# Attention in a two-layer graph network on one core: the order of the heads, and which of them goes into the shared third PSUM bank when

## The chip, the cores and the metric

The kernel runs on one core of one Trainium2 chip. Its time is the device time of one execution in microseconds (us). Before the change the median of three executions is 2405.86 us (2405.43 to 2407.07).

A core has several engines that run side by side, each with its own queue: TensorE (PE in the profile) multiplies matrices and writes its results to PSUM[...]; VectorE (DVE), ScalarE (ACT) and GpSimd (POOL) work element by element; SyncE (SP) issues the transfers (DMAs). An engine takes its instructions in the order in which they were written. Between engines, a semaphore tells one that another has finished.

## The reference, cut to what matters

There are 128 graphs of 128 nodes with 512 features each. Layer 0 is graph attention with 8 heads of 64 units, layer 1 a hypergraph convolution with a hidden width of 1024; each is added to its input and normalized. The change is in layer 0, in the product of the attention weights with the features:

```python
feats = jnp.einsum('bnf,hfu->bhnu', X, W)
e_self = jnp.einsum('bhnu,hu->bhn', feats, a_self)
e_neigh = jnp.einsum('bhnu,hu->bhn', feats, a_neigh)
dense = jax.nn.leaky_relu(e_self[..., :, None] + e_neigh[..., None, :], negative_slope=0.2)
dense = dense + NEG_BIG * (1.0 - A[:, None, :, :])
att = jax.nn.softmax(dense, axis=-1)
out = jnp.einsum('bhij,bhju->bhiu', att, feats) + b[None, :, None, :]
...
x = _layernorm(x + _L0_gnn_ref(x, adj, ...), axis=-1)
x = _layernorm(x + _L1_gnn_ref(x, adj, ...), axis=-1)
```

## The kernel before

**Pairs.** The 128 graphs are taken two at a time: 64 pairs, p = 0 to 63. All work of a pair is cut into steps, small functions such as `attend_pair(p, s)`, where `s` holds the pair's tiles. A step is declared with a lag and a time: `@step(2, 24.1, since=1, until=LAST)` puts it at (p + 2) x 38.6 + 24.1 on a clock that serves only for ordering. At the end of the kernel all steps of all pairs are sorted by that number and called; so several pairs are under way at once, and the order of each engine's queue is the order of the calls. The start and the last pairs have times and functions of their own.

**Attention of one pair.** The scores of both graphs lie in one tile `nb`, half a graph (four heads) at a time: GpSimd adds the mask (`masked`, line 589), ScalarE applies the leaky ReLU (line 605), VectorE takes the largest (line 611), ScalarE the exponential (line 619). The product needs the exponentials transposed. For that a graph's half of `nb` is written to DRAM (`e_write`, line 623: ed<-nb) and read back by blocks of 32 rows (`e_read`, line 631: four transfers eb<-ed), and VectorE transposes the blocks (`e_transpose`, line 640: eT<-eb), four heads in one instruction. There are four of these per pair: first graph's heads 0 to 3 and 4 to 7 (times 16.6 and 16.65), second graph's heads 0 to 3 and 4 to 7 (21.5 and 21.55).

**The product.** For each graph and head, `attend_pair` (line 703) multiplies the transposed exponentials `eT` with the features `ft`, which have a column of ones appended, so that each head gives 64 columns of results and one column with the sum of the weights: 65 columns. Each head is done in two matmuls of 64 output rows, and in the profile each of these is two records. A bank holds 512 fp32 columns, so seven heads (455 columns). Heads 0 to 6 of the first graph go into `pav_0`, those of the second into `pav_1`, and head 7 of both (`HB`) into a shared third bank, `pav_2`. `pav_2` is reserved in an earlier step (`attend_rest`, time 20.9), ahead of the first product of layer 1's second weights (pyX, time 21.0); `pav_0` and `pav_1` are reserved in `attend_pair`. All banks come from one pool of eight, `psum`. The order of the matmuls is: head 7 of both graphs, then heads 0 to 6 of the first, then heads 0 to 6 of the second.

**The evictions.** `attended_pair` (time 26.3, lines 734 and 735) takes the reciprocal of each sum and multiplies the results with it into `y`, in three instruction pairs on VectorE: `pav_2` first, then `pav_0`, then `pav_1`. `residual` (line 751) applies the ReLU and adds the input, `moments` (lines 759 and 760) and `rstds` (line 767, GpSimd) make the statistics of the layer norm, `first_shift` and `first_output` (lines 785 to 794, ScalarE) apply it to `y`, and `propagate` (pz, on TensorE) is the first use of `y`.

**Around the product.** On TensorE the last part of the feature product of the next pair (pfX, pfW) stands ahead of the attention, and products of layer 1's second weights (pyX, pyY, pyW) stand behind it; the helper of those matmuls is line 97. On VectorE, `f_sum` (line 509), `spread_rows` (line 542) and `x_transpose` (line 385) of other pairs stand between the last `e_transpose` and the evictions. Pairs 0 and 63 use `attend` and `attended`, with four heads to a bank, in place of the functions that are changed.

Of the kernel before, what the change touches and what calls it, by code (L numbers as in the profile page):

```python
# [20 lines left out]
def kernel(  # L21
# [67 lines left out]
    def bank(name):  # L89
        return psum.tile([P, HALF], F32, tag="bank", name=name)  # L90
# [120 lines left out]
    for i in range(2):  # L211
        t = const.tile([P, 2, H, UW + 1], F32, name=f"ft{i}")
# [103 lines left out]
    def step(lag, time, since=0, until=PAIRS):  # L316

        def keep(fn):
            steps.append((lag, time, fn.__name__, range(since, until), fn, ()))
            return fn  # L320
        return keep
# [364 lines left out]
    HB = H - 1  # L686

    @step(2, 20.9, since=1, until=LAST)
    def attend_rest(p, s):
        s["pav", 2] = bank(f"pav_{p}_2")  # L690

    @step(2, 24.1, since=1, until=LAST)
    def attend_pair(p, s):

        rest = s["pav", 2][:, :2 * (U + 1)].rearrange("p (g u) -> p g u", g=2)
        to = [(rest[:, g, :], g, HB) for g in range(2)]
        for g in range(2):
            t = s["pav", g] = bank(f"pav_{p}_{g}")
            to += [(t[:, h * (U + 1):(h + 1) * (U + 1)], g, h) for h in range(HB)]
        for t, g, h in to:  # L700
            for c in range(2):
                rows = slice(c * P // 2, (c + 1) * P // 2)
                nc.tensor.matmul(  # L703
                    t[rows], s["eT"][:, g, h, rows], s["ft"][:, g, h, 2:], start=True, stop=True,
                )
# [17 lines left out]
    @step(2, 26.3, since=1, until=LAST)  # L723
    def attended_pair(p, s):
        y = s["y"] = work.tile([P, 2, F], F32, tag="y", name=f"y_{p}")
        rden = small.tile([P, 2, H], F32, tag="rden2", name=f"rden_{p}", bufs=2)
        heads = y.rearrange("p g (h u) -> p g h u", h=H)
        rest = s["pav", 2][:, :2 * (U + 1)].rearrange("p (g u) -> p g u", g=2)
        for r, t, dst in [(rden[:, :, HB], rest, heads[:, :, HB, :])] + [
            (rden[:, g, :HB],  # L730
             s["pav", g][:, :HB * (U + 1)].rearrange("p (h u) -> p h u", h=HB),
             heads[:, g, :HB, :]) for g in range(2)
        ]:
            nc.vector.reciprocal(r, t[:, :, U])
            nc.vector.tensor_tensor(
                dst, t[:, :, :U], r.unsqueeze(2).to_broadcast(list(dst.shape)), op=ALU.mult
            )
# [538 lines left out]
```

## Time and profile before

| What | Value |
|---|---|
| median of three executions | 2405.86 us (2405.43 to 2407.07) |
| the profiled execution's own time | 2395.3 us |
| its span, first to last instruction | 2393.4 us |
| mean granted TensorE clock | 0.996 of full speed |
| PE (TensorE matmul) | busy 99% of the span |
| DVE (VectorE) | 87% |
| POOL (GpSimd) | 76% |
| ACT (ScalarE) | 64% |
| matmul records of attention, line 703 | 3968, for 62 pairs |
| reciprocals and multiplications of attended_pair | 186 each |
| bytes moved | 347.09 MB, mean 145 GB/s |

The profile is of one execution. Its page gives each engine's busy time, the chain of work that ended last, and the costliest groups of instructions. The trace behind it can be asked for more: the waits (who waited for whom, with total, number and longest), and the timeline, which lists instructions in order of time as start, length, engine, line, operation, what is written and read, and how many were merged in the row; in brackets stands how long the engine was idle before, and what ended that. A busy share is of the engine's whole span; the ends of matmuls are modelled, so a busy PE is not PE at its peak.

### The profile page before, as it was taken

How to read it: one execution, taken by the hardware profiler on the slowest of the kernel's cores; microseconds unless marked ns; L12 is line 12 of the kernel's file. 1: busy time of each engine (PE TensorE's matmuls, PEld its weight loads, DVE VectorE, ACT ScalarE, POOL GpSimd, SP SyncE). 2: the span in 40 equal slices, each digit the busy share in tenths (PEclk: the TensorE clock that was granted, in tenths of full speed). 3: DMA queues.
4: the chain of work that ended last, by engine and by line, in shares of the span. 5: the costliest groups of instructions: out<-in, count | busy, mean ns of one | idle time of the engine just before them, and what ended most of it. 6: DMA issues, size and time to landing. Idle time of an engine off the chain costs nothing.

```text
span 2393.4 us, 80729 instructions
## 1 busy us (share of the span) xinstructions
PE 2360.8 (99%) x32309; PEld 2026.8 (85%) x32309; DVE 2089.6 (87%) x4456; ACT 1528.5 (64%) x4481; POOL 1825.6 (76%) x2060
## 2 busy tenths in 40 slices
PE   7899999999999999999999999999999999999998
PEld 6788887888888888888888888888888888888886
DVE  7989888898898898898898888988988988988975
ACT  4565765756667667667667666666676676676662
POOL 5877786777877877877877778778778778778774
PEclk9999999999999999999999999999999999999999
DMA  6555454555554555555545555544545555555541
GB/s 197 133 148 150 143 144 134 159 143 147 151 148 144 149 148 148 151 143 154 144 142 157 141 147 155 146 146 147 150 143 153 147 150 139 148 156 140 149 128 37
DMA packets 431134, 347.09 MB, mean 145 GB/s; under 512 B 151440, under 2 KB 380328, under 8 KB 430760
## 3 DMA queue, kind: packets, MB, share of 16 engines
q1 hardware_dynamic: 427288, 337.46, 49.5%
q8 instruction: 256, 4.19, 0.7%
q10 hardware_dynamic: 3472, 4.47, 0.6%
q14 instruction: 118, 0.97, 0.2%
HBM read 239.08 MB, written 102.73 MB: 143 GB/s over the span
## 4 chain that ended last, share of the span: by engine, by line
PE 89%; DMA 4%; DVE 3%; ACT 1%; POOL 1%; issue 1%; SPq 1%; DVEq 0%; POOLq 0%; ACTq 0%
PE phX L97 17%; PE pyX L97 17%; PE pfX L97 8%; PE pyW L97 8%; PE phW L97 8%; PE pav L703 5%; PE phY L97 4%; PE pz L97 4%; PE pfW L97 4%; PE pq L97 4%; PE pyY L97 4%; PE pfY L97 2%; DMA ed<-nb 1%; PE pd L97 1%; DMA nb<-rd 1%
## 5 line engine op out<-in xcount | busy, mean ns | idle before, releaser
L344 ACT COPY py<-pyX 128x257 f32<-128x257 f32 x189 | 70.7, 374 | 538.5 <-PE pyX L97 465.6
L97 PEld LDWEIGHTS phX<-zS,w_sb 128*64 128x64 f32 x6144 | 350.6, 137 | 36.3 <-POOL ft L742 23.1
L97 PE MATMUL phX<-zS,w_sb 128*64 128x128 f32 x6144 | 373.4, 273 | 2.6 <-ACT ph L344 2.6
L904 POOL TENSOR_TENSOR sq<-sq 128x512 f32<-128x512 f32 (+2 forms) x384 | 343.9, 896 | 20.1
L589 POOL TENSOR_TENSOR nb<-nb,neg 128x512 f32<-128x512 f32 x256 | 319.9, 1284 | 23.1 <-DMA nb<-rd 12.7
L605 ACT ACTIVATE nb<-nb,ft 128x128 f32<-128x128 f32 x1020 | 325.1, 392 | 13.7 <-POOL nb L589 13.7
L619 ACT ACTIVATE nb<-nb,nm 128x128 f32<-128x128 f32 x1024 | 319.4, 392 | 4.2 <-DVE nm L611 4.0
L767 POOL TENSOR_TENSOR rso<-veo,mhalf 128x2 f32<-128x2 f32 x63 | 44.2, 701 | 338.4 <-DVE veo L765 338.4
L97 PE MATMUL pyX<-w_sb,hS 128*64 128x257 f32 x2016 | 245.1, 380 | 0.0
L97 PE MATMUL pyX<-w_sb,h 128*64 128x257 f32 x2016 | 243.7, 379 | 0.5 <-ACT py L344 0.5
L97 PE MATMUL pyW<-w_sb,hS 128*64 128x256 f32 x2016 | 243.3, 378 | 0.0
L881 ACT ACTIVATE h<-h,vecs 128x128 f32<-128x128 f32 x768 | 239.4, 394 | 2.0 <-DVE h L866 1.4
L611 DVE TENSOR_REDUCE nm<-nb 128x4 f32<-128x512 f32 x256 | 175.2, 684 | 48.8 <-ACT nb L605 46.2
L97 PEld LDWEIGHTS pyX<-w_sb,h 128*64 128x64 f32 x2016 | 173.7, 136 | 46.2 <-ACT py L344 0.9
L97 PEld LDWEIGHTS pyW<-w_sb,hS 128*64 128x64 f32 x2016 | 174.7, 136 | 43.6 <-issue 0.3
L742 POOL TENSOR_TENSOR ft<-ft,b_bc 128x512 f32<-128x512 f32 x128 | 203.9, 1613 | 6.1 <-ACT ft L533 6.1
L97 PEld LDWEIGHTS pyX<-w_sb,hS 128*64 128x64 f32 x2016 | 168.7, 137 | 38.7 <-issue 0.8
L640 DVE STREAM_TRANSPOSE eT<-eb 128x512 f32<-128x512 f32 x252 | 163.5, 685 | 5.7 <-DMA eb<-ed 4.7
L805 DVE SCALAR_TENSOR_TENSOR o<-y,b_bc 128x512 f32<-128x512 f32 x128 | 164.7, 1325 | 0.0
L1006 DVE SCALAR_TENSOR_TENSOR y<-y,rsh,bw_bc 128x512 f32<-128x512 f32 x126 | 150.1, 1229 | 14.9 <-POOL rsh L1002 14.9
L469 POOL TENSOR_TENSOR hS<-h 128x512 f32<-128x512 f32 x126 | 162.1, 1287 | 0.0
L892 ACT ACTIVATE sq<-h 128x512 f32<-128x512 f32 x256 | 160.6, 629 | 2.1
(178 smaller groups left out, 5672.4 us busy)
## 6 DMA issues: line engine op xcount, KB each, us to landing
nb<-rd SPq DMA_DIRECT2D x127, 512.0 KB, 5.6
ed<-nb SPq DMA_DIRECT2D x126, 512.0 KB, 3.4
eb<-ed SPq DMA_DIRECT2D x504, 128.0 KB, 2.9
x<-in_x_dram SPq DMA_DIRECT2D x64, 512.0 KB, 4.0
out_dram<-o SPq DMA_DIRECT2D x63, 512.0 KB, 2.9
xb<-in_x_dram SPq DMA_DIRECT2D x248, 128.0 KB, 5.5
a<-in_adj_dram SPq DMA_DIRECT2D x64, 128.0 KB, 2.4
w<-in_adj_dram SPq DMA_DIRECT2D x128, 64.0 KB, 5.0
```

The costliest lines, as they stand in the source:

```text
L97: nc.tensor.matmul(to[rows], lhs[:, rows], rhs, start=start, stop=stop, skip_group_check=True)
L469: engine.tensor_tensor(t[:, i], in0, in1, op=op)
L589: nc.gpsimd.tensor_tensor(t, t, neg[:, :, None, :].to_broadcast([P, NB, HH, B]), op=ALU.add)
L605: nc.scalar.activation(t, t, AF.Prelu, bias=s["ft"][:, g, h, 0:1], alpha=SLOPE)
L611: nc.vector.tensor_reduce(s["nm"][:, g, hs], scores(p, s, g, hs).rearrange("p b h j -> p h b j"), AX.XY, ALU.max, negate=True,)
L619: nc.scalar.activation(t, t, AF.Exp, bias=s["nm"][:, g, h:h + 1])
L640: nc.vector.transpose(s["eT"][:, g, hs, :].rearrange("p h (b i) -> p h b i", b=NB), s["eb", g][:, :, hs, :].rearrange("p b h j -> p h b j"),)
L742: nc.gpsimd.tensor_tensor(t, t, b0_bc.rearrange("p (h u) -> p h u", h=H), op=ALU.add)
L805: nc.vector.scalar_tensor_tensor(s["o"][:, g, :], s["y"][:, g, :], 2.0, b2_bc, op0=ALU.mult, op1=ALU.add)
L881: nc.scalar.activation(dst[:, k, :], src[:, k, :], AF.Relu, bias=b1_sb[:, c:c + 1])
L892: nc.scalar.activation(s["sq"][:, g, q * KH // 2:(q + 1) * KH // 2, :], hid(s, g, q), AF.Square, scale=DH ** -0.5,)
L904: nc.gpsimd.tensor_tensor(t[:, :n, :], t[:, :n, :], t[:, n:2 * n, :], op=ALU.add)
```

## The change

The early step now reserves the bank of the first graph's heads 0 to 6 (`pav_0`), and `attend_pair` reserves `pav_1` and `pav_2`. The matmuls are issued in the order of the heads: heads 0 to 6 of the first graph into `pav_0`, its head 7 into `pav_2`, then heads 0 to 6 of the second graph into `pav_1`, and its head 7 into `pav_2`. The evictions follow the same order: `pav_0`, `pav_1`, and `pav_2` last. The number, the shapes and the operands of all instructions stay. Steps of pairs 0 and 63 are not touched.

```diff
     @step(2, 20.9, since=1, until=LAST)
     def attend_rest(p, s):
-        s["pav", 2] = bank(f"pav_{p}_2")
+        s["pav", 0] = bank(f"pav_{p}_0")
...
-        to = [(rest[:, g, :], g, HB) for g in range(2)]
+        to = []
         for g in range(2):
-            t = s["pav", g] = bank(f"pav_{p}_{g}")
+            t = s["pav", g]
             to += [(t[:, h * (U + 1):(h + 1) * (U + 1)], g, h) for h in range(HB)]
+            to.append((rest[:, g, :], g, HB))
...
-        for r, t, dst in [(rden[:, :, HB], rest, heads[:, :, HB, :])] + [
+        for r, t, dst in [
             (rden[:, g, :HB],
              s["pav", g][:, :HB * (U + 1)].rearrange("p (h u) -> p h u", h=HB),
              heads[:, g, :HB, :]) for g in range(2)
-        ]:
+        ] + [(rden[:, :, HB], rest, heads[:, :, HB, :])]:
```

At the head of `attend_pair` stands the new reservation:

```python
s["pav", 1], s["pav", 2] = (bank(f"pav_{p}_{g}") for g in (1, 2))
```

## The prediction

> **What bounds the kernel now.** I read the page first, then the waits of TensorE, then the timeline of one steady pair, and then the places where the waits of TensorE in attention lie.
>
> ```profile
> span 2393.4 us, 80729 instructions
> ...
> PE 2360.8 (99%) x32309; PEld 2026.8 (85%) x32309; DVE 2089.6 (87%) x4456; ACT 1528.5 (64%) x4481; POOL 1825.6 (76%) x2060
> ...
> PE 89%; DMA 4%; DVE 3%; ACT 1%; POOL 1%; issue 1%; SPq 1%; DVEq 0%; POOLq 0%; ACTq 0%
> ```
>
> TensorE is busy for 99% of the span and carries 89% of the chain that ended last. So a change of order can gain only where TensorE waits, and can lose only where it makes TensorE wait. The list of TensorE's waits, cut to those that touch attention (line 703) and the next consumer of its result (pz), has per row the total, the number and the longest:
>
> ```profile
> PE pz L97 <- ACT y L794: 4.0, 1, 4.0
> PE pav L703 <- DVE eT L640: 4.0, 2, 2.3
> ...
> PE pav L703 <- POOL hS L469: 0.6, 1, 0.6
> ```
>
> Three waits in 62 pairs, 4.6 us in all. The steady pair shows why there are no more. From its timeline (start, length, engine, work), first VectorE's transposes of the exponentials, then the 64 matmul records (two for each of the 32 matmuls), the next product, and VectorE's evictions:
>
> ```profile
> 1031.33 1.29 DVE L640 STREAM_TRANSPOSE eT<-eb 128x512 f32<-128x512 f32 x2
> ...
> 1032.77 2.07 PE L703 MATMUL pav<-ft,eT 128*64 128x65 f32 x64
> ...
> 1034.63 1.95 PE L97 MATMUL pyX<-w_sb,hS 128*64 128x257 f32 x16
> ...
> 1034.74 0.13 DVE L734 RECIPROCAL rden<-pav 128x2 f32<-128x2 f32 x1
> ```
>
> The last transpose (second graph, heads 4 to 7) ends at 1031.33 + 1.29 = 1032.62; attention starts 0.15 us later and is not interrupted: 64 records in 1034.63 - 1032.77 = 1.86 us, 29 ns each. VectorE comes to the first eviction at 1034.74, when all matmuls have been issued. The waits are these, pair 1 and pair 8:
>
> ```profile
> 114.58 0.32 PE L703 MATMUL pav<-ft,eT 128*64 128x65 f32 x4
> ...
> 115.17 1.30 DVE L640 STREAM_TRANSPOSE eT<-eb 128x512 f32<-128x512 f32 x2 [1.31 <-DMA eb<-ed]
> ...
> 116.62 1.97 PE L703 MATMUL pav<-ft,eT 128*64 128x65 f32 x60 [1.72 <-DVE eT L640]
> ...
> 373.12 0.31 PE L703 MATMUL pav<-ft,eT 128*64 128x65 f32 x4
> ...
> 374.30 1.30 DVE L640 STREAM_TRANSPOSE eT<-eb 128x512 f32<-128x512 f32 x2 [2.23 <-DMA eb<-ed]
> ...
> 375.75 3.47 PE L703 MATMUL pav<-ft,eT 128*64 128x65 f32 x60 [2.32 <-DVE eT L640]
> ```
>
> Four records run (the first graph's head 7), then the second graph's head 7 waits for the very last transpose and 60 records queue behind it, 28 of which belong to the first graph and were ready. Pair 2 is alike (0.62 us; its releaser is named POOL, but its last transpose ends at 153.68 and TensorE goes on at 153.82, the same 0.15 us as in the others).
>
> **What the Trainium skill says.** "TensorE: Matmul & The Clock Gate", section on the measured speedup of packing: matmuls are strictly first in, first out, only weight loads are pulled ahead. The trace agrees: 60 records stand behind one. The same page, "What's actually happening" in Part 1: an idle window of about 3.4 us halves the array's clock. Here the 60 records after 2.32 us of idle time took 3.47 us instead of 1.97, and those after 1.72 us of idle time did not slow down; a shorter gap than the page's window was enough. "Perfetto Trace Analysis", section on the Tensor Engine's instruction: a wait is served in a queue ahead of execution, so one that is already satisfied need not show. The trace agrees: pyX, which waits for two engines, starts 16 to 25 ns after the record before it. "VectorE: DVE Perf Modes", "The DRAIN you can't avoid": a semaphore between two instructions adds nothing to the flush. The trace differs: in this stage a dependent instruction starts 0.03 us after the end of the one before, an independent one 0.08 us ahead of it.
>
> **The change part by part.**
> *Matmuls.* The same 32 per pair, 64 records of 29 ns; nothing added or removed. The instruction lists of both kernels show pav_0 x14, pav_2 x2, pav_1 x14, pav_2 x2 in place of pav_2 x4, pav_0 x14, pav_1 x14, and no other move on TensorE; ScalarE, GpSimd and the DMA queue keep their lists. Cost in a steady pair: 0.
> *The wait for the last transpose.* It moves from the third matmul to the 25th (second graph's head 4); the wait for the second graph's first transpose stands at the 17th. Behind the last one, 16 records stay instead of 60: 44 x 29 ns = 1.3 us less per late pair.
> Pair 1: first graph 114.58 to 115.51; first transpose of the second graph ends at 115.82, + 0.15 = 115.97; four heads to 116.43; last transpose at 116.47 + 0.15 = 116.62; 16 records to 117.08, against 118.39 for the next product now: 1.3 us.
> Pair 2: again 1.3 us if its transposes stay where they are, but then it only keeps what pair 1 gave; if they move with TensorE, its own 0.6 us comes on top. Both ends: 1.3 to 1.9 us for the two pairs. I take 1.6.
> Pair 8: the 60 records and the slow clock end at 379.03; then they would end at 375.75 + 0.47 = 376.22: 2.8 us (2.4 if the clock still falls). But that wait comes of one transfer (the write of the exponentials took 7.04 us in the chain, where the other pairs' took about 5), once in 62 pairs: other executions may have none, or several. I take half: 1.4.
> Pairs at which nothing is late gain nothing.
> *New waits.* By the lists, TensorE's waits in the block become 7 semaphores instead of 6. Below: no cost, as at pyX. Above: if each pair showed one wait at the measured 0.15 us of a real release, 62 x 0.15 = 9 us. I take 0, since nothing in the present block shows a satisfied wait. If the cover goes, the whole rest of TensorE's queue is behind it.
> *Banks.* pav_0 takes the bank that was reserved early (the step attend_rest), pav_1 and pav_2 those of the pair reserved at 24.1. All former readers were over: the list names no VectorE wait for them now, only TensorE's own. 0. The bank that used to be free after the two-head eviction is freed 0.4 us later; its next user is eight reservations on, 10 us away: 0.
> *Evictions.* Three reciprocal and multiply pairs, as now (0.13 + 0.29 and twice 0.20 + 0.62). The first needs pav_0, written 28 records = 0.8 us after the start, and VectorE comes 1.97 us after the start: no wait; the last needs pav_2, complete at about 2.1, and VectorE comes to it at about 3.5. Added: the residual of the first graph now reads what the instruction just before it wrote; 0.03 + 0.08 = 0.11 us per pair on VectorE. Behind it wait the moments, GpSimd's power, ScalarE's y and TensorE's pz. ScalarE's y ends at 1041.92 + 1.51 = 1043.43 and pz starts at 1045.04: 1.6 us to spare, which hides 0.11. If it did not, 62 x 0.11 = 7 us would be the upper bound. The same 0.11 us can reach the next transposes, which in the present order have only some 0.12 us to spare (115 ns from the start of the block to its fifth record, plus 150, less the 146 ns of a release); in the new order the last transpose has 1.3 us more. So it is hidden there too.
> *Pairs 0 and 63* use another function and stay.
>
> Sum: - 1.6 - 1.4 + 0 = - 3.0 us, ends - 1.3 and - 4.7. The profiled execution took 2395.3 us (span 2393.4 and 1.9 around it); it would take 2392.3. The median of the runs shown is 2405.86, 10.6 us above the profiled one, and no view says where these lie. I subtract from the median: 2402.9.
>
> **The rivals.**
> *Nothing is gained.* TensorE arrives earlier, and waits elsewhere: the pairs up to 8 have small waits for ScalarE's zT and for transfers that start from VectorE, and VectorE still waits for the late transfer in the same place. Against it: those waits are relative to TensorE's own feature product, so they move with it, and from pair 15 on the pairs follow each other at 36.37 us without a gap. Time: 2405.9.
> *Many pairs are late when no profile is taken.* The 10.6 us are 0.17 us for each of 62 pairs, and the slack of the last transpose is only 0.12 us. Were VectorE a little later there, TensorE would wait in each pair, and the new order would hide all of it. For it: the thin slack. Against it: in the profile it holds in nearly every pair. Taking some two thirds of the 10.6: 2405.9 - 1.6 - 7 = 2397.
> *Slower: a wait becomes visible in the middle of the block.* Now the waits stand at its head; the new 17th and 25th matmuls carry waits, one for three engines. If handling one opened a gap of 0.15 us per pair, 9.1 us less the 3.0 gained gives 2412. It decides from (4.8 + 3.0)/62 = 0.13 us per pair. Against it: pyX's 16 to 25 ns.
> That the change does not do what it says is excluded by the lists.
>
> **How the numbers follow.** My forecast has 0.60, nothing gained 0.17, many late pairs 0.15, slower 0.08. 0.2% (4.8 us) is about what a measurement of this kernel can tell from no change; so my forecast counts as the same but for the case that two or more late transfers are hidden, 0.10 of its 0.60. Faster: 0.15 + 0.10 = 0.25. Same: 0.50 + 0.17 = 0.67. Slower: 0.08. The range leaves out the slower case and the better half of the many late pairs: 2397.5 to 2407.0, the top being the highest run shown, since no gain at all is within it.
>
> **What would show it.** Right: in pair 1, the block runs 32 records on without a break, then waits, and the next product starts 1.3 us earlier; no pair has 60 records behind a transpose; the distance of steady pairs stays 36.37 us; the first eviction is of seven heads and does not wait. Wrong: a gap between the 16th and 17th or the 24th and 25th matmul of steady pairs; pz waiting for y in steady pairs; or a time below 2398, which would say that unprofiled runs wait here much more often.

## The result, and the profile after

The changed kernel takes 2398.01 us (median of 13 executions, 2394.48 to 2402.39); the kernel before, run beside it, takes 2404.24 us (median of 13, 2399.03 to 2407.07). The ratio is 0.9978, with a 95% interval of 0.9970 to 0.9987: 5.3 us less (3.1 to 7.2); the two medians lie 6.2 us apart. The forecast was 3.0 us less, 2402.9, with a range of 2397.5 to 2407.0.

The single profiled executions say the opposite: 2398.11 us after, against 2395.3 before. The profiled execution of before was faster than all 13 timed ones of the same kernel. So the two traces must not be subtracted from each other; what each shows place by place can still be compared.

The page of the kernel after, the lines that answer to those shown of before:

```profile
span 2396.3 us, 80729 instructions
...
PE 2361.6 (99%) x32309; PEld 1898.1 (79%) x32309; DVE 2087.9 (87%) x4456; ACT 1528.2 (64%) x4481; POOL 1823.2 (76%) x2060
...
PE 81%; DMA 8%; DVE 4%; ACT 3%; POOL 2%; SPq 1%; issue 1%; DVEq 0%; POOLq 0%; ACTq 0%
```

The number of instructions and TensorE's busy time are the same. TensorE still bounds the kernel. Transfers have more of the chain than in the first trace (8% against 4%), but that need not be an effect of the change: a second trace of the kernel before, from experiment 1, has PE 79% and DMA 9%.

A steady pair after, from the timeline (start, length, engine, line, work):

```profile
1033.39 1.29 DVE L640 STREAM_TRANSPOSE eT<-eb 128x512 f32<-128x512 f32 x2
...
1034.86 2.03 PE L705 MATMUL pav<-ft,eT 128*64 128x65 f32 x64
...
1036.73 1.91 PE L97 MATMUL pyX<-w_sb,hS 128*64 128x257 f32 x16
1036.80 0.19 DVE L736 RECIPROCAL rden<-pav 128x7 f32<-128x7 f32 x1
...
1038.53 0.29 DVE L737 TENSOR_TENSOR y<-pav,rden 128x128 f32<-128x128 f32 x1
1038.85 1.08 DVE L753 SCALAR_TENSOR_TENSOR y<-y,x 128x512 f32<-128x512 f32 x1
```

The block takes 1036.73 - 1034.86 = 1.87 us, as against 1.86 before, in one piece. The first eviction is of seven heads, and VectorE comes to it when all matmuls have been issued. The residual starts 0.03 us behind the instruction that it depends on.

Pairs 2, 4 and 9 after, in the kernel's own count of p. Where the prediction and the expectations speak of late pairs, they count one less: `attend_pair` runs for p = 1 to 62, its first block stands at 74.5 us, and the block near 114.6 us, their pair 1, is that of p = 2. Their pairs 1, 2 and 8 are thus p = 2, 3 and 9. From here on the numbers are those of the kernel.

```profile
114.84 1.13 PE L705 MATMUL pav<-ft,eT 128*64 128x65 f32 x32
115.64 1.30 DVE L640 STREAM_TRANSPOSE eT<-eb 128x512 f32<-128x512 f32 x2 [1.52 <-DMA eb<-ed]
116.50 1.19 PE L705 MATMUL pav<-ft,eT 128*64 128x65 f32 x32 [0.53 <-DVE eT L640]
...
117.52 1.91 PE L97 MATMUL pyX<-w_sb,hS 128*64 128x257 f32 x16
...
188.96 1.30 DVE L640 STREAM_TRANSPOSE eT<-eb 128x512 f32<-128x512 f32 x2 [1.17 <-DMA eb<-ed]
189.12 2.04 PE L705 MATMUL pav<-ft,eT 128*64 128x65 f32 x64
...
373.64 1.10 PE L705 MATMUL pav<-ft,eT 128*64 128x65 f32 x32
374.34 1.30 DVE L640 STREAM_TRANSPOSE eT<-eb 128x512 f32<-128x512 f32 x2 [1.96 <-DMA eb<-ed]
375.20 1.19 PE L705 MATMUL pav<-ft,eT 128*64 128x65 f32 x32 [0.46 <-DVE eT L640]
```

In pair 2 the first graph's 32 records run at once. From the end of the last transpose (115.64 + 1.30 = 116.94) to the next product (117.52) it is 0.58 us; before it was 118.39 - 116.47 = 1.92. In pair 4 the last transpose ends at 190.26, 1.14 us after the block began, and the block runs through in one piece: a late pair that costs nothing now. In pair 9 the last transpose ends 2.0 us after the block began; TensorE waits 0.46 us, and its second half keeps the full rate (1.19 us for 32 records).

The waits of TensorE after, those for attention (line 705) and for zT, ScalarE's copy of pz that the first hidden product reads:

```profile
PE phX L97 <- ACT zT L831: 6.1, 9, 1.5
...
PE pav L705 <- DVE eT L640: 1.7, 4, 0.5
```

### The profile page after: what moved, and what is told of

Its sections match the earlier page's. It is cut to its first block, busy times and chain, and to the rows that moved or that the text cites. A ratio compares the mean times of both kernels' runs of the same rounds, so it can differ in the third digit from the quotient of the medians.

```text
span 2396.3 us, 80729 instructions
## 1 busy us (share of the span) xinstructions
PE 2361.6 (99%) x32309; PEld 1898.1 (79%) x32309; DVE 2087.9 (87%) x4456; ACT 1528.2 (64%) x4481; POOL 1823.2 (76%) x2060
## 4 chain that ended last, share of the span: by engine, by line
PE 81%; DMA 8%; DVE 4%; ACT 3%; POOL 2%; SPq 1%; issue 1%; DVEq 0%; POOLq 0%; ACTq 0%
PE phX L97 16%; PE pyX L97 15%; PE pfX L97 8%; PE phW L97 8%; PE pyW L97 7%; PE phY L97 4%; PE pfW L97 4%; PE pav L705 4%; PE pq L97 4%; PE pz L97 4%; PE pyY L97 4%; DMA ed<-nb 3%; DMA nb<-rd 2%; PE pfY L97 2%; ACT nb L605 1%; DMA rd<-rows 1%
## 5 line engine op out<-in xcount | busy, mean ns | idle before, releaser
L906 POOL TENSOR_TENSOR sq<-sq 128x512 f32<-128x512 f32 (+2 forms) x384 | 343.1, 894 | 20.1
L97 PEld LDWEIGHTS pyX<-w_sb,h 128*64 128x64 f32 x2016 | 149.8, 137 | 70.0 <-ACT py L344 0.9
L97 PEld LDWEIGHTS pyW<-w_sb,hS 128*64 128x64 f32 x2016 | 149.8, 137 | 69.2 <-issue 0.7
L97 PEld LDWEIGHTS pyX<-w_sb,hS 128*64 128x64 f32 x2016 | 144.7, 137 | 60.9
```

Of the source, the lines that this page charges most:

```text
L97: nc.tensor.matmul(to[rows], lhs[:, rows], rhs, start=start, stop=stop, skip_group_check=True)
L906: nc.gpsimd.tensor_tensor(t[:, :n, :], t[:, :n, :], t[:, n:2 * n, :], op=ALU.add)
```

## The experiments

**1. How often is a pair late? The kernel before, once more.** No edit.

> The kernel before, unchanged, timed against itself and profiled once more. Late-pair theory (the gain is about 1.3 us for each of a few early pairs whose last transpose comes late, and their number changes from one execution to the next): ratio 1.000, and the new trace shows other late pairs than the first one (which had 1, 2 and 8), between two and six of them in all, all within the first 20 pairs. Rival 'every pair waits a little': many or all of the 62 pairs show a gap after the fourth record of the attention block.

Ratio 0.9997 (0.9987 to 1.0006), median 2402.78 us. Its waits of TensorE:

```profile
PE pav L703 <- DVE eT L640: 5.3, 4, 2.1
...
PE pav L703 <- POOL hS L469: 3.8, 2, 2.0
PE phX L97 <- ACT zT L829: 3.7, 7, 1.1
```

Attention waits 9.1 us in six pairs here, against 4.6 us in three in the first trace. They stand at 116.9, 191.0, 229.4, 342.6, 418.7 and 1186.5 us: five at the start, one in the middle, which was not expected. The row that names GpSimd is the same wait: in both of its cases TensorE goes on 0.15 us after the last transpose. All other pairs from p = 2 on run without a gap, so the rival of a small wait in each pair falls. The DMA queue shows where one of these comes from (pair 8; the write of the first graph's exponentials, its four reads, the second graph's write and reads):

```profile
322.82 0.34 SPq L623 DMA_DIRECT2D ed<-nb  x1
329.99 1.73 SPq L631 DMA_DIRECT2D eb<-ed  x4
331.83 0.37 SPq L623 DMA_DIRECT2D ed<-nb  x1
336.56 1.73 SPq L631 DMA_DIRECT2D eb<-ed  x4
```

The reads wait until the first write has landed and go out 7.2 us after it, and the second write stands behind them in the queue.

**2. The order of the matmuls alone.** From the kernel after, the evictions go back to their old order:

```diff
-        for r, t, dst in [
+        for r, t, dst in [(rden[:, :, HB], rest, heads[:, :, HB, :])] + [
...
-        ] + [(rden[:, :, HB], rest, heads[:, :, HB, :])]:
+        ]:
```

> The new reservation of banks and the new order of matmuls, with the evictions in the old order (shared bank first). Late-pair theory: the whole gain is in the matmul order, so 0.997 to 0.999 (about -5 us), the same as with the full change; VectorE's first eviction waits some 0.1 to 0.2 us for the end of the block, which is hidden. Rival 'the order of the evictions does it': 1.000.

Ratio 0.9973 (0.9963 to 0.9982), 2397.26 us: the whole gain. Attention waits 3.3 us in this trace:

```profile
PE pav L705 <- DVE eT L640: 3.3, 4, 1.3
```

**3. The order of the evictions alone.** From the kernel before, the same edit the other way.

> The old order of matmuls and reservation, with the evictions in the new order (shared bank last). Late-pair theory: nothing, 1.000 (within 2 us), with 60 records still queued behind the third matmul in late pairs. Rival 'the order of the evictions does it': 0.998.

Ratio 0.9992 (0.9985 to 0.9998), 2401.68 us. That is 2 us less, at the edge of what the unchanged kernel shows against itself in experiment 1; whether it is anything stays open. The waits are those of the old order:

```profile
PE pav L703 <- DVE eT L640: 9.3, 6, 3.0
...
PE phX L97 <- ACT zT L829: 4.1, 6, 1.4
```

**4. The reservation of the banks.** From the kernel after, the shared bank is reserved early again, and the other two at the attention's step:

```diff
     def attend_rest(p, s):
-        s["pav", 0] = bank(f"pav_{p}_0")
+        s["pav", 2] = bank(f"pav_{p}_2")
...
-        s["pav", 1], s["pav", 2] = (bank(f"pav_{p}_{g}") for g in (1, 2))
+        s["pav", 0], s["pav", 1] = (bank(f"pav_{p}_{g}") for g in (0, 1))
```

> The new orders of matmuls and evictions, with the banks reserved as before (the shared bank early, the two others at the attention's step). Theory: reservation plays no part, since every bank's former reader is long done: the same as the kernel after, 0.997 to 0.999. If the early reservation of the first graph's bank is part of the gain: nearer to 1.000, with a gap ahead of the attention block.

Ratio 0.9986 (0.9978 to 0.9994), 2399.02 us. The interval overlaps that of the change, attention waits 1.9 us, and no gap stands ahead of the block. No part of the reservation is shown; the estimate lies 1.9 us above that of the change, and the times alone do not exclude a part of that size.

**5 and 6. Every pair made late.** One more instruction on VectorE ahead of the second graph's transposes, in the kernel before and in the kernel after:

```diff
     def e_transpose(p, s, g, q):
...
+        if (g, q) == (1, 0):
+            late = small.tile([P, 1], F32, tag="late", name=f"late_{p}")
+            nc.vector.tensor_reduce(late, b2_bc, AX.X, ALU.add)
```

> The kernel before, with one more VectorE instruction ahead of the second graph's two transposes of each pair (a reduction of 512 columns whose result is not used, 0.68 us), so that each pair's last transpose is made late. Late-pair theory: the slack of the last transpose is 0.12 us, so TensorE waits some 0.55 us with 60 records behind it in each of 61 pairs: + 30 to + 35 us, near 2436, and the trace shows a gap after the fourth record in nearly every pair. Rival 'the order of evictions, or something else than this wait, makes the difference': about the same small loss as in the kernel after with the same instruction.

> The kernel after, with the same added VectorE instruction. Late-pair theory: the last transpose now comes 0.66 us later but is needed only 1.4 us after the start of the block, so steady pairs show no wait: + 0 to + 4 us on the kernel after (the late pairs of the start are later still), 2398 to 2402, ratio to the kernel before 0.997 to 1.000. Rival: as much slower as the kernel before with the same instruction.

In the old order 2424.15 us, ratio 1.0084 (1.0069 to 1.0099). In the new one 2403.39 us, ratio 1.0002 (0.9991 to 1.0012). A steady pair in the old order, with the added instruction:

```profile
1041.31 0.67 DVE L641 TENSOR_REDUCE late<-b_bc 128x1 f32<-128x512 f32 x1
...
1041.90 1.29 DVE L643 STREAM_TRANSPOSE eT<-eb 128x512 f32<-128x512 f32 x2
1042.76 0.31 PE L706 MATMUL pav<-ft,eT 128*64 128x65 f32 x4
...
1043.34 1.97 PE L706 MATMUL pav<-ft,eT 128*64 128x65 f32 x60 [0.27 <-DVE eT L643]
```

And in the new order:

```profile
1038.60 0.67 DVE L641 TENSOR_REDUCE late<-b_bc 128x1 f32<-128x512 f32 x1
...
1039.19 1.29 DVE L643 STREAM_TRANSPOSE eT<-eb 128x512 f32<-128x512 f32 x2
1040.07 2.03 PE L708 MATMUL pav<-ft,eT 128*64 128x65 f32 x64
```

The last transpose ends 0.43 us (old) and 0.41 us (new) after the block began. The old order stops after four records, in nearly every pair; the new one runs through. Same lateness, 20.8 us of difference. The waits of the old order:

```profile
PE pav L706 <- DVE eT L643: 23.0, 60, 2.1
```

The 20 us that the old order loses are less than the 30 to 35 expected. The starts of the blocks show why. Steady pairs follow each other at 36.85 us instead of 36.37, so each of them loses 0.49 us (the transpose moved by 0.58 us and not by 0.66). From the 21st block to the last that is 20.1 us more than in experiment 1. Over the first 20 pairs the two traces take the same time (747.3 and 746.9 us): there TensorE had waits anyway, and the added one took their place (that for zT fell to 1.2 us from 3.7). The new order loses 5 us rather than 0 to 4, all of it in the first 20 pairs (747.8 us, after 741.9); its waits for zT rose to 8.5 us. Its steady pairs keep their 36.37 us.

**7. The lateness taken away at its source.** From the kernel before, from pair 2 on the second graph's write is issued ahead of the first graph's reads:

```diff
-        at(2, (6.2, 10.9)[g], e_write, g, since=1)
+        at(2, (6.2, 10.9)[g], e_write, g, since=1, until=2)
+        at(2, (6.2, 9.95)[g], e_write, g, since=2)
         at(2, (10.0, 14.9)[g], e_read, g, since=1)
```

> The kernel before, with the second graph's write of the exponentials ahead of the first graph's reads on the DMA queue (from pair 2 on), so that it no longer waits until the first write has landed. If the lateness comes of this queue (a slow first write holds back the second one), the late pairs from 2 on vanish from the old order of heads too: 0.997 (some 6 us less), as much as the change itself gives. If the lateness comes of the transfers' own times or of ScalarE, it stays at 1.000.

Ratio 0.9957 (0.9945 to 0.9969), 2393.09 us: 11 us less (10.3 by the ratio), about twice what the change gives, with the old order of heads. TensorE's waits:

```profile
PE phX L97 <- ACT zT L830: 5.7, 8, 1.2
...
PE pav L704 <- DVE eT L640: 1.1, 4, 0.3
```

The waits do not account for all of it. This trace is 9.8 us shorter than the mean of those of experiments 1 and 3. Attention waits 8.1 us less and zT 1.8 us more, which leaves 3.5 us; 2.2 us of the 9.8 lie before the first block and after the last one. What shortened these, in this one trace, stays open.

**8. Both.** The same edit in the kernel after.

> The kernel after, with the earlier write of the second graph's exponentials. Late-pair theory: the two edits remove the same waits, so they do not add up: beyond the 11.0 us of the early write on the old order of heads, the new order has only pair 1 and some 0.8 us of small waits left to hide, 1 to 2 us: 2391 to 2393, ratio to the kernel before 0.995. If the new order gained by something else than late transposes, it would bring its own 5 us again: 2387, 0.993.

Ratio 0.9958 (0.9943 to 0.9973), 2393.82 us: the new order adds nothing that can be seen once the transposes are in time. The two intervals leave room for some 4.6 us either way, so by the times alone a second gain of 5.3 us is only just excluded. The waits say more: in this trace, the slowest of the seven executions, attention (line 706) has none, and zT 6.7 us. The pair that the expectation left to the new order is p = 2, which the early write reaches too. One late transfer is left, in pair 9, and meets the first graph's transposes, which stand ahead of the features on VectorE:

```profile
370.82 1.30 DVE L640 STREAM_TRANSPOSE eT<-eb 128x512 f32<-128x512 f32 x2 [2.25 <-DMA eb<-ed]
...
375.33 1.68 PE L97 MATMUL pfW<-w_sb,xS 128*64 128x264 f32 x8 [2.23 <-DVE ft L509]
```

**9. More time for the second graph.** From the kernel after, its eight heads are a step of their own behind pyX:

```diff
+    @step(2, 27.75, since=1, until=LAST)
+    def attend_second(p, s):
+        attend_graph(p, s, 1, s["pav", 2][:, :2 * (U + 1)].rearrange("p (g u) -> p g u", g=2))
...
-    @step(2, 26.3, since=1, until=LAST)
+    @step(2, 28.0, since=1, until=LAST)
     def attended_pair(p, s):
```

> From the kernel after: the second graph's eight heads are issued one product later, behind pyX (1.74 us), and the evictions' step moves behind that. Late-pair theory: the last transpose gets 1.74 us more, so that the attention waits of pairs 1, 7, 8 and 9 in the trace of after (0.5 us at most) vanish: about 2 us less than the kernel after, 2396, ratio to the kernel before near 0.997. Against it: VectorE waits some 0.9 us per pair for the second graph, which leaves 0.4 of the 1.6 us that y has to spare; if that is not enough, pz waits for y in most pairs and the kernel is slower than before, 2410 or more.

Ratio 0.9982 (0.9975 to 0.9990), 2398.38 us. Attention no longer waits in these pairs at all, as expected, but the kernel is not faster than the one after: zT still waits 4.8 us, pyW waits 0.9 us for VectorE, which is new, and steady pairs follow each other at 36.40 us instead of 36.37, some 2 us in all. pz does not wait for y in steady pairs.

**10 and 11. The waits for zT.** From the kernel after, ScalarE's leaky ReLU of the first graph's second half goes behind the first zT; then, in a second kernel that has the early write too, the first exponentials also go behind the first copy of the hidden product:

```diff
-        ((0, 0), 31.0, (1, 33.2), (1, 36.1), 3.9, 16.6), ((0, 1), 32.2, (1, 37.3), (1, 38.75), 4.6, 16.65),
+        ((0, 0), 31.0, (1, 33.2), (1, 36.1), 4.05, 16.6), ((0, 1), 32.2, (2, 1.15), (2, 1.2), 4.6, 16.65),
```

> The kernel after, with ScalarE's first eviction of pz (zT) one leaky ReLU earlier in its queue. The trace of after shows ten waits of TensorE for zT, 5.4 us from pair 1 on, each of at most 1.5 us, where ScalarE stood behind a late read of the scores (nb). One leaky ReLU is 1.28 us, so all but some 0.5 us should go: about 4 us less than the kernel after, 2394, ratio to the kernel before 0.996. Against it: if the scores' chain is late there anyway, the wait turns up at the next transposes, and nothing is gained on the kernel after (0.9978).

> The new order of heads, the early write, ScalarE's first zT one leaky ReLU earlier, and the first graph's first exponentials behind ScalarE's copy of the first hidden product, which was the copy that came 0.43 us late in every pair in the earlier trial. The copy then stands 0.8 us ahead of its old place, so that wait is gone, and the zT waits (5.7 us in the trace with the early write) fall below 1 us: 2387 to 2389, ratio 0.993. If the first exponentials' delay makes the first write late instead, attention or zT waits return: 2392 or more.

Both missed. The first (with 3.9 in place of 4.05) took 2431.14 us, ratio 1.0116 (1.0103 to 1.0130). Its longest row of TensorE's waits, beside what is left of the zT waits:

```profile
PE phX L97 <- ACT ph L344: 31.4, 63, 3.0
...
PE phX L97 <- ACT zT L831: 2.1, 2, 1.5
```

ScalarE now sits idle until pz is ready (1.02 us in a steady pair), and the copy of the first hidden product comes 0.43 us late in nearly every pair. The second took 2403.71 us, ratio 1.0006 (0.9996 to 1.0015): zT waits 1.0 us, close to what was expected, but the copy is waited for 6.7 us in 23 places. Most last transposes are 0.4 to 0.5 us late, yet attention (`attend_pair`) does not wait at all: the new order hides them. The first 20 pairs are the quickest of all traces (737.2 us), and the loss lies behind them, some 10 us against experiment 8. In neither kernel did such a move of ScalarE's work around pz bring anything.

## Why the prediction was right, point by point

**The mechanism held.** The order of the matmuls carries the gain (experiments 2 to 4; parts of up to 2 us of the other two edits are not excluded), it acts through the place of the wait for the last transpose (5 and 6), and without late transposes it is worth nothing that can be seen (8). Nor were fewer pairs late by chance: the last transpose ended over 0.3 us after the block's start in 3, 6 and 6 pairs of the traces with the old matmul order (first, experiments 1 and 3), and in 8, 10 and 6 of those with the new one (after, experiments 2 and 4). Late pairs are not fewer than before; they cost less. That matmuls are served first in, first out stands on the page of the Trainium skill that the prediction names, "TensorE: Matmul & The Clock Gate", but in "The mechanism" of Part 3 and not in the section on the measured speedup. The traces agree, with up to 60 records behind one late transpose.

**44 records of 29 ns per late pair** was right in pair 2: the way from the last transpose to the next product went from 1.92 to 0.58 us, 1.34 us less against the predicted 1.3. Pair 4 shows the other case, in which the lateness is below 1.3 us and vanishes whole.

**The term that was mis-sized is the one of the rare late transfer**, "I take half: 1.4". It was built on one profiled execution, which had three late pairs and turned out to be the fastest seen of that kernel. Two other traces of the old order of matmuls show six each. The balance in microseconds:

| TensorE waits for | old matmul order: first trace, experiment 1, 3 | new matmul order: after, experiment 2, 4 |
|---|---|---|
| the transposes (attend_pair's line) | 4.6, 9.1, 9.3 | 1.7, 3.3, 1.9 |
| zT | 1.3, 3.7, 4.1 | 6.1, 5.5, 5.2 |

From the two ordinary traces of the old order, 9.2 us, to the mean of the new one, 2.3 us, is 6.9 us less; the waits for zT rise from 3.9 to 5.6, which gives 1.7 back. The 5.2 us left agree with the 5.3 measured. But the first trace is left out here because its execution was unusually fast; with it the same balance gives 2.8 us. So this is a balance from a few traces and not a proof of each term.

**"Nothing is gained, TensorE waits elsewhere"** was thus true of a quarter of the gain, at zT. The argument against it, that those waits only move with TensorE, was too strong. They rise to 5.7 us with the old order of heads too, once the transposes are in time (experiment 7).

**That the time fell in the range is in part luck.** The 2398.01 us lie 0.5 us above its lower end, and the gain of 5.3 us lies above both ends of the sum, 1.3 and 4.7, though its interval (3.1 to 7.2) takes in the upper one. Of the 4.9 us between forecast and result, 1.6 come of the starting value (2405.86 from three executions, 2404.24 from thirteen) and 3.2 of the gain (6.2 between the medians, 3.0 forecast). The sign of being wrong, a time below 2398, was missed by 0.01 us. What it stood for, more waits than the first trace shows, is the case, though in the first pairs and not in most.

**"Many pairs are late when no profile is taken"** was wrong as a mechanism. The 10.6 us between the profiled execution of before and the median came of the choice of executions: the later medians of before lie at 2402.8 to 2404.2, and experiment 1's own profiled execution (2403.73) with its six waits lies among them. The thin slack of 0.12 us was real, as experiment 5 shows, but steady pairs keep it.

**New waits, banks and evictions at nothing** held: the block takes 1.87 us against 1.86, steady pairs follow each other at 36.37 us as before, they have no gap at the 17th or 25th matmul, the residual follows 0.03 us behind its operand, and pz does not wait for y in steady pairs. That the clock falls after a long stop in the block did not come up in the kernel after: its stops there are below 0.6 us, and the full rate follows them.

## What to carry to other kernels

In a queue that is served in order, put the work whose operands arrive last at the end of its block. Here it cost nothing in steady pairs, and each late arrival was hidden, in whole or in part, by what stood ahead of it. But look first for what makes it late; here one transfer, queued behind another's wait, was worth about twice as much as the order, and both together no more than the one. And where a few irregular waits carry the effect, count them in several executions before pricing them.

## What the runs showed that was not expected

TensorE's waits for late transposes lie nearly all in the first 11 of 62 pairs (single ones at 1186 us in experiment 1 and at 2276 us in experiment 3). One in pair 9 comes back in five of the six traces of the balance above (at 375.8, 379.9, 375.2, 375.8 and 375.6 us in the first trace, experiment 3, after, and experiments 2 and 4); experiment 1 lacks it. What slows the transfers there stays open.

A stop of 2.32 us halved TensorE's rate (60 records in 3.47 us) in the first trace, where the granted clock of these 60 records was 0.53 of full speed. One of 2.04 us in experiment 1 slowed it less. But the longest, 2.98 us in experiment 3, did not slow it at all, with a granted clock of 1.00 behind it. Experiment 1, and below it experiment 3:

```profile
342.62 2.42 PE L703 MATMUL pav<-ft,eT 128*64 128x65 f32 x60 [2.04 <-POOL hS L469]
```

```profile
379.88 1.97 PE L703 MATMUL pav<-ft,eT 128*64 128x65 f32 x60 [2.98 <-DVE eT L640]
```

So the length of the stop alone does not decide, and the prediction's "a shorter gap than the page's window was enough" describes its one pair and is not a rule.
